# Residual rows with bias laid out in tile order in DRAM during the scores, for a two-layer attention kernel on one Trainium2 core

## Chip, cores and metric

The kernel runs on one core of a Trainium2 chip. The time is the device time of one execution in microseconds (us). Three runs of the kernel before gave 3094.94, 3099.14 and 3100.99 us; the median is 3099.14 us. One further execution was recorded by the hardware profiler and took 3099.78 us. All views below are of that execution, and times within it count from its first instruction. The engines are called PE (TensorE; PEld is its weight load), DVE (VectorE), ACT (ScalarE), POOL (GpSimd) and SP (SyncE, which here only issues DMAs).

## What is computed

There are N = 2708 rows of D = 1024 features in x and a matrix adj of N x N integers. Two attention layers follow each other, each on the normalised rows and each with a residual:

```
h = max(layernorm(x), 0)
f = h @ Wf + bf ;  g = h @ Wg + bg
e = max(f @ g.T, 0)
attention = softmax(where(adj > 0, e, -9e15), axis=1)
x = x + attention @ (h @ W + bW)              # layer 0

h = max(layernorm(x), 0)
hW = h @ W1 ;  e = leaky_relu(hW @ a1 + (hW @ a2).T, 0.2)
attention = softmax(where(adj > 0, e, -9e15), axis=1)
x = x + max(attention @ hW, 0)                # layer 1
```

All is in 32-bit floats. The rows of attention add up to 1, so the kernel adds bW to the residual row instead of to h @ W. The sum x + bW for the rows of layer 0 is what this change is about.

## The kernel before

**Panels and tiles.** The output rows are worked on in five panels of 512 rows (panels 0 to 4). Panels 0 and 1 have 64 rows more each and panel 2 has 20 more; these 64 + 64 rows form a tile called MONO and the 20 rows one called TINY. A tile has 128 rows in four groups of 32: group g of tile t of a panel holds rows that begin at `start_of_tile(t) + 128 * g`, so that the rows of one tile are not neighbours in x. `places[t]` lists, for each group, the partitions and the first row. `pairs` joins two tiles; there are ten pairs, q = 0 to 9, and MONO with TINY comes after them.

**Stages of a layer-0 panel p.** (1) `project_q` (PE names qx, qy, qz) makes the operand B of the scores. (2) `scores` multiplies it with the transposed rows of all ten pairs. For each q it loads four blocks As (hs_d to SBUF, in `product`, matmul at L1378), builds the mask for pair q + 1 (integers of adj are loaded, converted and turned on DVE, stored to mk_d by GpSimd), and adds mask and maximum on DVE. (3) The softmax runs beside later matmuls. (4) `aggregate` (gx, gy, gz, gv at L661) multiplies the weights with h; the division by the row sums is at L977, partly on GpSimd. (5) `project` (px, py, pz, pv at L1267) multiplies with W and hands each half tile to `finish0`, which adds it to the residual row, stores the sum to x1_d and makes the normalised rows for layer 1. The products are cut in Strassen's manner into seven (M1 to M7). Panel p's projection comes after its aggregation for p = 0, 1, 2 and 4; panel 3's comes after the scores of panel 4.

**The residual rows.** `finish0(p).start` runs when `project` begins, after the first four loads of W and ahead of all others. For each tile of the panel it takes two half rows of 512 columns, x_res, in SBUF. `load_rows_of` fills them by eight loads of 32 rows x 512 columns (64 KB) from x; MONO takes four of 64 rows, TINY sixteen small ones. Then two DMAs on GpSimd add the bias row, repeated on 128 partitions, into x_res (L1612; for TINY eight at L1607). `go` and `join` add the projected rows to it.

**What sets the order.** All loads go through `load`, which issues on SP and keeps the order of the program. Stores go through `store` on GpSimd; a scheduler may move them unless they are kept in order too. `nc.hold` keeps DVE's instructions in order during the scores. Side work (statistics of finished rows, masks, quarter sums) waits in the lists `later` and `lazy` and is taken by `behind(us)` after each product. Tiles in SBUF come from pools: `slots` (54 buffers, x_res among them) and `strm` (12 buffers: As, W blocks w, hc, adj_i, g1 and g2). A load waits for the release of its buffer, and so does everything behind it on SP. The built order also shows that a DMA waits for the one eight places before it among the DMAs of the same engine.

Of the kernel before, what the change touches and what calls it, by code (L numbers as in the profile page):

```python
# [57 lines left out]
def kernel(  # L58
# [66 lines left out]
    def slot(name, shape=(P, WX), dt=FP):  # L125
        return slots.tile(list(shape), dt, tag="slot", name=name)
# [10 lines left out]
    def load(o, i):  # L137
        for a, b in in_16(o, i):
            tc.keep_in_program_order(nc.sync.dma_start(a, b))
# [146 lines left out]
    def by_quarters(a, r, e):  # L286

        return [(slice(B32 * g, B32 * g + NY), a[r:r + NY, e * W + g * P:e * W + (g + 1) * P]) for g in range(P // B32)]
# [1064 lines left out]
    def scores(p, B):  # L1353

        w = width[p]
        h = w // 2
        lo, hi = slice(0, h), slice(h, w)
        fetch, convert, turn = makers[p]
        rb = slot("rb")
        if p == 0:  # L1360
            spread(rb, columns_of(p, r_[:, first_col[p]:]))
        else:
            row_on_all(rb, r_d[p], p)
        acc = slot("acc")
        S = [None] * NT
        rates = (0.6, 1.0, 0.65, 0.65, 0.65)
        lefts = {}

        def product(q, m, ps, start):
            n, i = P, BY_SCORES.index(m)  # L1370
            if i % 2 == 0:
                t = stream("As", (P, 2, NH, P))
                lefts[q] = t
                k = min(2, 7 - i)
                load(t[:, :k].rearrange("p m c j -> p (m c j)"),
                     hs_d[q][:, i:i + k].rearrange("p m c j -> p (m c j)"))
            for c in range(NH):
                nc.tensor.matmul(ps[:n, :h], lefts[q][:, i % 2, c, :n], B[m][c // 2][:, c % 2, :h],  # L1378
                                 start=(start and c == 0), stop=(c == NH - 1), skip_group_check=True)

        def finish(q, s, k):

            n, mk = once(q, k), mk_sb[p, q]
            nc.vector.scalar_tensor_tensor(s[:, :w], s[:, :w], 0.0, mk[:, k, :w], op0=OP.max, op1=OP.add)
            if q == 0 and k == 0:
                nc.vector.tensor_copy(acc[:, :w], s[:, :w])
            else:
                nc.vector.tensor_tensor(acc[:n, :w], acc[:n, :w], s[:n, :w], OP.max)
            if q in known:
                raise_max(p, q, k, mk[:n, k, :w])  # L1390

        def last(q, sb, Z, m1):

            n = P
            product(q, M4, Z, False)
            add(sb[:n, lo], Z[:n, :h], m1[:n, lo])
            finish(q, sb, 1)
            mk_sb.pop((p, q))
            behind(rate, True)

        nc.hold = ("vector",)
        left_over = None
        for q in range(NQ):
            n = P
            make_until(q + 2)
            rate = 1.3 if NQ - 1 not in made else rates[p]
            if q + 2 <= LEFT:
                fetch(q + 2)
            sa, sb = slot("Sa"), slot("Sb")
            S[pairs[q][0]], S[pairs[q][1]] = sa, sb  # L1410
            X, Y, Z = (bank(f"s{k}") for k in "xyz")
            m1, t = slot("sm1"), slot("st")
            product(q, M1, X, True)
            for s in (lo, hi):
                add(m1[:n, s], X[:n, :h], rb[:n, s])
            if left_over:
                left_over()
            product(q, M6, Z, True)
            add(t[:n, lo], Z[:n, :h], m1[:n, hi])
            behind(rate, True)  # L1420
            product(q, M5, Y, True)
            add(t[:n, hi], Y[:n, :h], m1[:n, hi])
            if q + 1 <= LEFT:
                convert(q + 1)
            behind(rate, True)
            product(q, M2, X, False)
            add(sa[:n, lo], X[:n, :h], rb[:n, lo])
            if q + 1 <= LEFT:
                turn(q + 1, 0)
            behind(rate, True)  # L1430
            product(q, M7, Z, False)
            add(sb[:n, hi], Z[:n, :h], t[:n, hi])
            if q + 1 <= LEFT:
                turn(q + 1, 1)
            behind(rate, True)
            product(q, M3, Y, False)
            add(sa[:n, hi], Y[:n, :h], t[:n, lo])
            finish(q, sa, 0)
            behind(2 * rate, True)
            left_over = lambda q=q, sb=sb, Z=Z, m1=m1: last(q, sb, Z, m1)  # L1440

        sm, st = slot("Sa"), slot("Sb")
        S[MONO], S[TINY] = sm, st
        X, Y, Z = (bank(f"s{k}") for k in "xyz")
        m1, zs = slot("sm1"), slot("sz")
        t = stream("As", (P, 2, NH, P))
        load(t.rearrange("p e c j -> p (e c j)"), hsl_d.rearrange("p e c j -> p (e c j)"))

        def part(ps, e, m, start):
            for c in range(NH):  # L1450
                nc.tensor.matmul(ps[:, :h], t[:, e, c], B[m][c // 2][:, c % 2, :h], start=(start and c == 0),
                                 stop=(c == NH - 1), skip_group_check=True)
        part(X, 0, M1, True)
        add(m1[:, hi], X[:, :h], rb[:, hi])
        left_over()

        for c in range(NH):
            for g, (e, m) in enumerate(((0, M1), (1, M2), (0, M5), (1, M3))):
                nc.tensor.matmul(Z[B32 * g:B32 * (g + 1), :h], tinyT[:, e, c], B[m][c // 2][:, c % 2, :h], start=(c == 0),
                                 stop=(c == NH - 1), skip_group_check=True)  # L1460
        nc.scalar.copy(zs[:, :h], Z[:, :h])
        part(X, 1, M2, False)
        add(sm[:, lo], X[:, :h], rb[:, lo])
        behind(rate, True)
        part(Y, 0, M5, True)
        part(Y, 1, M3, False)
        add(sm[:, hi], Y[:, :h], m1[:, hi])
        finish(LEFT, sm, 0)
        for s, pick in zip((lo, hi), picks):
            V = bank("sv")  # L1470
            nc.tensor.matmul(V[:, :h], pick, zs[:, :h], start=True, stop=True)
            add(st[:, s], V[:, :h], rb[:, s])
        finish(LEFT, st, 1)
        mk_sb.pop((p, LEFT))
        behind(rate, True)
        nc.hold = ()
        return S, acc
# [110 lines left out]
        nc.gpsimd.memset(t, 0.0)  # L1588
        return [t[:, e] for e in range(2)]

    def bias_of_W(o, n, k):
        return bass.AP(tensor=bw.tensor, offset=bw.offset + o, ap=[[0, n], [1, k]])

    def finish0(p):
        xs, seen = {}, {}

        def start(ts):
            for t in ts:
                if p == NP - 1:
                    first_mask[t] = load_mask(0, *pair_of[t])  # L1600
                if t == TINY:
                    xs[t] = halves_of_tiny("x_res")
                    for e in range(2):
                        for ps, i in by_quarters(x, places[TINY][0][1], e):
                            load(xs[t][e][ps], i)
                        for g, (ps, _) in enumerate(by_quarters(x, 0, e)):
                            nc.gpsimd.dma_start(xs[t][e][ps], bias_of_W(e * W + g * P, NY, P), accum_op=OP.add)  # L1607
                    continue
                xs[t] = row_halves("x_res", t == MONO)
                load_rows_of(t, xs[t], x)  # L1610
                for e in range(2):
                    nc.gpsimd.dma_start(xs[t][e], bias_of_W(e * W, P, W), accum_op=OP.add)  # L1612

        def go(t, e, c):
            add(xs[t][e], c, xs[t][e])
            if t == TINY:
                for ps, o in by_quarters(x1_d[t], 0, e):
                    store(o, xs[t][e][ps])
            else:
                store(x1_d[t][:, e * W:(e + 1) * W], xs[t][e])  # L1620
            seen[t] = seen.get(t, 0) + 1
            if seen[t] == 2 and t == TINY:
                put(0.5, lambda: rows_of_tiny())
            elif seen[t] == 2:
                rows_done(t, xs[t])

        def rows_of_tiny():
            xs[TINY] = row_halves("x_res")
            for e in range(2):
                nc.gpsimd.memset(xs[TINY][e], 0.0)  # L1630
                for ps, _ in places[TINY]:
                    nc.gpsimd.dma_start(xs[TINY][e][ps], x1_d[TINY][:, e * W:(e + 1) * W])
            rows_done(TINY, xs[TINY])

        def join(t, e, c):
            add(xs[t][e], xs[t][e], c)
        return start, join, go
# [199 lines left out]
```

## Time and profile before

| what | value |
|---|---|
| median of three runs | 3099.14 us |
| profiled execution | 3099.78 us |
| its span, first to last instruction | 3098.0 us |
| DVE, ACT and POOL busy | 2070.7, 463.2, 506.3 us |
| mean granted clock of PE | 0.989 of full speed |
| mean DMA rate | 247 GB/s |
| scores of panels 1, 2, 3, 4 | about 661, 1074, 1452, 1771 us to 812, 1212, 1590, 1902 us |
| projections of panels 0 to 4 begin | about 611, 1012, 1399, 1902, 2085 us |

How to read the views. "Busy" is the time in which an engine executed; waiting and issuing DMAs are not counted. The waits of an engine name the instruction that waited, what released it, and the total, the number and the longest. A timeline row has the start, the length, the engine, the line and the operation, and in brackets the idle time before it with its releaser. A row of a stretch has the length, the busy time of PE, PEld, DVE, ACT and POOL (each with its number of instructions), the mean granted clock of PE as a share of full speed, the mean busy share of the 16 DMA engines, and their rate in GB/s. In names, a buffer's number is left out, so x_d stands for every x1_d tile; "SPq" is SP's DMA queue.

### The profile page before, as it was taken

The numbers are of one execution on the slowest core, as the hardware profiler recorded it, in microseconds if no ns is written. First come the engines' busy times: TensorE is split into PE (matmuls) and PEld (weight loads), VectorE is DVE, ScalarE is ACT, GpSimd is POOL, SyncE is SP. The second block draws the span as 40 slices with busy tenths as digits, with TensorE's granted clock in tenths as the row PEclk, the third lists the DMA queues.
The fourth block names the chain that finished last, engine by engine and source line by source line (L and its number), as shares of the span: only waits on it lengthen the run. The fifth ranks groups of instructions, "written<-read, shape, count | busy, mean of one in ns | idle before, by whom it ended". The sixth has DMA issues, their size and how long they took to land.

```text
span 3098.0 us, 41680 instructions
## 1 busy us (share of the span) xinstructions
PE 3002.8 (97%) x14630; PEld 2298.1 (74%) x14630; DVE 2070.7 (67%) x4615; ACT 463.2 (15%) x817; POOL 506.3 (16%) x786
## 2 busy tenths in 40 slices
PE   8998999899999999999999999997999999999998
PEld 4576777657877588885888886783777969879694
DVE  5767693776651596716975277766968768887853
ACT  3420020010110101101011001301222121212200
POOL 1421101310011110214101001141202010020202
PEclk9999999999999999999999999998999999999999
DMA  6999967998565796758967577789667868888896
GB/s 225 291 257 254 301 247 253 309 274 229 178 238 153 217 260 223 244 158 241 278 199 255 164 217 234 237 266 350 229 216 249 274 202 296 287 269 294 264 297 246
DMA packets 448577, 764.70 MB, mean 247 GB/s; under 512 B 175776, under 2 KB 262592, under 8 KB 448368
## 3 DMA queue, kind: packets, MB, share of 16 engines
q1 hardware_dynamic: 393008, 598.31, 62.0%
q0 software_dynamic: 55360, 163.73, 16.4%
q8 instruction: 116, 1.90, 0.3%
q14 instruction: 93, 0.76, 0.1%
HBM read 627.95 MB, written 133.91 MB: 246 GB/s over the span
## 4 chain that ended last, share of the span: by engine, by line
PE 71%; DVE 11%; DMA 7%; issue 7%; SPq 2%; POOL 1%; ACT 1%; POOLq 0%; DVEq 0%; ACTq 0%
PE sz L1378 6%; PE gx L661 6%; PE gy L661 6%; PE gz L661 5%; PE gz L1067 5%; PE pz L1267 4%; PE sx L1378 4%; PE sy L1378 4%; PE px L1267 4%; PE py L1267 3%; PE gx L1067 3%; PE gy L1067 3%; PE M_ps L574 3%; PE qz L661 2%; PE qx L661 2%
## 5 line engine op out<-in xcount | busy, mean ns | idle before, releaser
L1378 PE MATMUL sz<-B,As 128*128 128x288 f32 (+2 forms) x1200 | 293.5, 394 | 11.8 <-DVE st L45 8.8
L1378 PEld LDWEIGHTS sz<-B,As 128*128 128x128 f32 x1200 | 227.8, 191 | 61.8 <-DVE st L45 12.7
L1378 PE MATMUL sx<-B,As 128*128 128x288 f32 (+2 forms) x800 | 199.6, 392 | 6.4 <-DMA As<-hs_d 4.4
L1378 PE MATMUL sy<-B,As 128*128 128x288 f32 (+2 forms) x800 | 199.3, 392 | 2.3 <-DMA As<-hs_d 2.3
L661 PE MATMUL gz<-Sa,hc 128*128 128x288 f32 (+2 forms) x800 | 189.2, 397 | 6.3 <-DMA hc<-hg_d 6.3
L661 PEld LDWEIGHTS gz<-Sa,hc 128*128 128x128 f32 x800 | 153.8, 193 | 40.1 <-DMA hc<-hg_d 6.8
L1378 PEld LDWEIGHTS sx<-B,As 128*128 128x128 f32 x800 | 151.3, 190 | 40.1 <-DMA As<-hs_d 3.7
L1378 PEld LDWEIGHTS sy<-B,As 128*128 128x128 f32 x800 | 152.0, 190 | 33.4 <-issue 2.7
L1067 PE MATMUL gz<-quarter,hc 128*128 128x128 f32 (+2 forms) x1344 | 168.8, 279 | 3.8 <-DVE gT L45 3.7
L143 POOL DMA_DIRECT2D out_dram<-x_res x180 | 89.0, 501 | 482.1 <-DVE x_res L45 474.7
L1067 PEld LDWEIGHTS gz<-quarter,hc 128*128 128x128 f32 x1344 | 160.6, 191 | 5.1 <-DVE gT L45 4.6
L1267 PE MATMUL px<-w,gT 128*128 128x512 f32 x320 | 143.9, 602 | 7.5 <-DMA w<-in_L_gnn_W_dram 6.0
L1267 PE MATMUL pz<-w,ps 128*128 128x512 f32 x320 | 142.1, 594 | 0.8 <-DVE pt L45 0.8
L1267 PE MATMUL py<-w,ps 128*128 128x512 f32 x320 | 142.0, 593 | 0.0
L143 POOL DMA_DIRECT2D mk_d<-mask x55 | 35.8, 652 | 534.8 <-DVE mask L45 528.1
L1267 PEld LDWEIGHTS px<-w,gT 128*128 128x128 f32 x320 | 60.9, 193 | 80.9 <-issue 74.7
L1267 PEld LDWEIGHTS pz<-w,ps 128*128 128x128 f32 x320 | 60.2, 190 | 77.1 <-issue 70.7
L1267 PEld LDWEIGHTS py<-w,ps 128*128 128x128 f32 x320 | 60.5, 190 | 75.8 <-issue 73.9
L574 PE MATMUL M_ps<-wgT,wfT 128*128 128x512 f32 x256 | 113.5, 600 | 1.6 <-ACT hsT L45 1.6
L661 PE MATMUL gy<-T,hc 128*128 128x288 f32 (+2 forms) x480 | 111.6, 394 | 0.0
L977 POOL TENSOR_TENSOR gT<-gT,rr 128x2304 f32<-128x2304 f32 (+5 forms) x12 | 44.4, 3700 | 382.4 <-DVE rr L45 179.8
L661 PEld LDWEIGHTS gy<-T,hc 128*128 128x128 f32 x480 | 91.2, 190 | 19.5
(377 smaller groups left out, 5803.6 us busy)
## 6 DMA issues: line engine op xcount, KB each, us to landing
hc<-hg_d SPq DMA_DIRECT2D x175, 512.0 KB
As<-hs_d SPq DMA_DIRECT2D x150, 512.0 KB
hc<-hr_d SPq DMA_DIRECT2D x119, 512.0 KB
hc<-hs_d SPq DMA_DIRECT2D x112, 512.0 KB
w<-wt_d SPq DMA_DIRECT2D x96, 512.0 KB
w<-in_L_gnn_W_dram SPq DMA_DIRECT2D x72, 512.0 KB
md<-md_d SPq DMA_DIRECT2D x56, 512.0 KB
adj_i<-in_adj_dram SPq DMA_DIRECT2D x200, 128.0 KB
```

Source lines behind the costliest of these rows:

```text
L143: nc.gpsimd.dma_start(a, b)
L574: nc.tensor.matmul(ps, wfT[a][c // NH][:, c % NH, :], wgT[b][c], start=(c == 0), stop=(c == NC - 1))
L661: nc.tensor.matmul(ps[d], left(m, k, d), right(m, k), start=(start and k == 0), stop=(k == K - 1), skip_group_check=True)
L977: nc.gpsimd.tensor_tensor(of(e, s), of(e, s), by(s, k), OP.mult)
L1067: nc.tensor.matmul(ps[:, d], lhs[:, d * P:(d + 1) * P], inner_right(m, n, k), start=(start and k == 0 and d == 0), stop=(k == NK - 1), ski ...
L1267: nc.tensor.matmul(ps, left[i][m][:, k, :], w_[k], start=(start and k == 0), stop=(k == NH - 1), skip_group_check=True)
L1378: nc.tensor.matmul(ps[:n, :h], lefts[q][:, i % 2, c, :n], B[m][c // 2][:, c % 2, :h], start=(start and c == 0), stop=(c == NH - 1), skip_g ...
```

## The change

For panels 1 to 4 the sum x + bW is made in DRAM, in the order of the tiles, in the tensors x1_d[t], which before only took the result of layer 0. In the scores of panel p, at q = 2, GpSimd issues one DMA per tile that copies the tile's rows from x to x1_d[t] (two for MONO, one for TINY). At q = 6 it issues one accumulating DMA per tile that adds the bias row to x1_d[t]. Both are kept in GpSimd's order of the program. In `finish0.start` a tile is then loaded from x1_d[t] by two loads of 128 rows x 512 columns (256 KB) with no accumulate after them. TINY keeps its sixteen small loads, now from x1_d. Panel 0 stays as it was.

```diff
@@ scores(p, B)
             if q + 2 <= LEFT:
                 fetch(q + 2)
+            if p and q in (2, 6):
+                (copy_residual if q == 2 else bias_residual)(p)
@@ beside finish0
-    def bias_of_W(o, n, k):
-        return bass.AP(tensor=bw.tensor, offset=bw.offset + o, ap=[[0, n], [1, k]])
+    def tiles_of(p):
+        return list(full(p)) + ([MONO, TINY][p - 1:p] if p in (1, 2) else [])
+
+    def by_gpsimd(o, i, **k):
+        tc.keep_in_program_order(nc.gpsimd.dma_start(o, i, **k))
+
+    def copy_residual(p):
+        for t in tiles_of(p):
+            if t < MONO:
+                r = places[t][0][1]
+                by_gpsimd(x1_d[t].rearrange("(g r) c -> g r c", g=P // B32),
+                                    bass.AP(tensor=x.tensor, offset=x.offset + r * D, ap=[[P * D, P // B32], [D, B32], [1, D]]))
+            else:
+                for ps, r in places[t][:1] if t == TINY else places[t]:
+                    by_gpsimd(x1_d[t][:NY] if t == TINY else x1_d[t][ps],
+                                        x[r:r + ps.stop - ps.start, :])
+
+    def bias_residual(p):
+        for t in tiles_of(p):
+            n = NY if t == TINY else P
+            by_gpsimd(x1_d[t], bass.AP(tensor=bw.tensor, offset=bw.offset, ap=[[0, n], [1, D]]), accum_op=OP.add)
@@ finish0.start
                     for e in range(2):
-                        for ps, i in by_quarters(x, places[TINY][0][1], e):
+                        for ps, i in by_quarters(x1_d[t], 0, e):
                             load(xs[t][e][ps], i)
-                        for g, (ps, _) in enumerate(by_quarters(x, 0, e)):
-                            nc.gpsimd.dma_start(xs[t][e][ps], bias_of_W(e * W + g * P, NY, P), accum_op=OP.add)
                     continue
                 xs[t] = row_halves("x_res", t == MONO)
-                load_rows_of(t, xs[t], x)
+                if p == 0:
+                    load_rows_of(t, xs[t], x)
                 for e in range(2):
-                    nc.gpsimd.dma_start(xs[t][e], bias_of_W(e * W, P, W), accum_op=OP.add)
+                    if p == 0:
+                        nc.gpsimd.dma_start(xs[t][e], bass.AP(tensor=bw.tensor, offset=bw.offset + e * W, ap=[[0, P], [1, W]]),
+                                            accum_op=OP.add)
+                    else:
+                        load(xs[t][e], x1_d[t][:, e * W:(e + 1) * W])
```

## Prediction

> **What bounds the kernel now.** I read the page's busy shares first, then the waits of TensorE (PE), then, for the one long wait there, the timelines of PE and of SyncE's DMA queue (SP) and the stretches around it.
>
> ```profile
> PE 3002.8 (97%) x14630; PEld 2298.1 (74%) x14630; DVE 2070.7 (67%) x4615; ACT 463.2 (15%) x817; POOL 506.3 (16%) x786
> ...
> PE sz L1378 <- DVE st L45: 8.8, 8, 2.2
> PE mx_ps L849 <- DVE mx L45: 8.3, 1, 8.3
> ...
> PE gz L661 <- DMA hc<-hg_d: 6.3, 1, 6.3
> PE px L1267 <- DMA w<-in_L_gnn_W_dram: 6.0, 1, 6.0
> ```
>
> PE is busy for 3002.8 of 3098.0 us, so 95 us of idle is all that an edit without matmuls can touch. The waits (columns: total, times, longest) name one that the residual loads can cause: 6.0 us before px at L1267, the projection of layer 0, for a block of W. None is for x_res. The wait for hg_d belongs to panel 0, the 8.3 us for mx to the chain after the last tile of layer 0.
>
> ```profile
> 2085.15 3.60 PE L1267 MATMUL px<-w,gT 128*128 128x512 f32 x8
> 2088.59 3.60 PE L1267 MATMUL py<-w,ps 128*128 128x512 f32 x8
> 2098.14 6.29 PE L1267 MATMUL px<-w,gT 128*128 128x512 f32 x8 [5.96 <-DMA w<-in_L_gnn_W_dram]
> 2104.27 3.60 PE L1267 MATMUL pz<-w,ps 128*128 128x512 f32 x8
> ```
>
> This is panel 4. Eight matmuls take 3.44 us from start to start (2085.15 to 2088.59); those after the wait take 6.13 (2098.14 to 2104.27). So the wait costs 5.96 us and then 6.13 - 3.44 = 2.7 us more. The stretches show why, in the granted clock (second last but one column):
>
> ```profile
> 2092.00:2098.00 6.00, 0.18 (x1) 0.00 (x0) 1.99 (x3) 0.00 (x0) 0.86 (x1) 0.88 1.10 259
> 2098.00:2105.00 7.00, 6.86 (x10) 2.92 (x11) 0.53 (x1) 0.00 (x0) 0.00 (x0) 0.61 1.06 364
> ```
>
> The block was late because of SP, which issues in order:
>
> ```profile
> 2054.56 2.82 SPq L139 DMA_DIRECT2D w<-wt_d  x2
> 2057.47 1.45 SPq L139 DMA_DIRECT2D maskl<-mk_d  x1
> 2058.97 7.89 SPq L139 DMA_DIRECT2D x_res<-in_x_dram  x8
> 2067.05 0.34 SPq L139 DMA_DIRECT2D maskl<-mk_d  x1
> 2067.84 5.95 SPq L139 DMA_DIRECT2D x_res<-in_x_dram  x8
> 2074.08 0.34 SPq L139 DMA_DIRECT2D maskl<-mk_d  x1
> 2074.70 5.52 SPq L139 DMA_DIRECT2D x_res<-in_x_dram  x8
> 2080.38 0.34 SPq L139 DMA_DIRECT2D maskl<-mk_d  x1
> 2080.83 7.90 SPq L139 DMA_DIRECT2D x_res<-in_x_dram  x8
> 2088.77 1.82 SPq L139 DMA_DIRECT2D w<-in_L_gnn_W_dram  x2
> ```
>
> The 32 loads of 64 KB hold SP for 7.89 + 5.95 + 5.52 + 7.90 = 27.3 us; W goes out at 2088.77 and lands at 2098.0, 9.2 us later. [...]
>
> In the projections of panels 1 to 3 (stretches 1005 to 1075, 1390 to 1460, 1895 to 1955) PE is busy for 70.0 of 70, 68.6 of 70 and 60.0 of 60 us, with no wait for W: the same loads are hidden there.
>
> [...]
>
> **The change, part by part.**
>
> Removed on SP: 148 loads from x. Added: 50 loads from x1_d, 34 of 256 KB (16 small ones for TINY are exchanged one for one). For panel 4 it is 8 for 32. Loads of that size from x1_d exist in layer 1: 329 ns at the median to issue, 852 at most. In the built order SP's loads around them stand as before, so what holds SP is read from its waits: the third and fourth mask loads and the fourth tile wait until the first two pairs of quarter sums (hs_d<-hq) are stored. GpSimd issues those at 2059.8 and 2063.6, two each, 0.73 us apiece, and they land 6.9 us later (median), so by about 2072. Eight loads at 0.33 to 0.85 us are 3 to 7 us and end inside that. W for px goes out at about 2072, its buffer free since gz ended at 2064, and with the same 9.2 us lands at 2081 to 2082: ten us ahead of PE, which is there at 2092.03. So 5.96 + 2.7 = 8.7 us go.
>
> What is late next? The following blocks wait for buffers that gv frees between 2068 and 2085, the seventh for px at 2088.6 with 17 us to its use; loads in this stretch land in 9 to 10 us. So none. The 0.78 us wait for pt at 2108.64 stays, as VectorE must empty the bank first, and the 8.3 and 3.9 us at 2143 to 2157 hang on the last tile and move with it.
>
> Removed on GpSimd: 42 bias accumulates of panels 1 to 4 (34 of 256 KB, 0.94 us to issue at the median, and with panel 0's 42.8 us of waiting for loads). Nothing on PE waited for them; VectorE lost 2.5 us, beside PE's wait. Cost off the path: zero. In panels 1 and 2 the second scaling of gT (L977) no longer stands behind an accumulate; PE didn't wait for it either.
>
> Added on GpSimd: 19 copies at q = 2 and 18 accumulates at q = 6. By the nearest rows, 0.5 to 0.75 us to issue a store and 0.94 (to 2.25) for an accumulate: 3 us and 5 us (to 11) per panel. Queued behind are mask stores, and in panels 1 and 2 stores of layer-1 rows (hr_d). GpSimd is idle for 10 to 13 us before each late mask store, and the bias comes 50 us after the copy it waits for, so this is hidden. If hr_d<-g is late, SP waits for its stream buffer (7.4, 1.9 and 14.7 us in the scores of panels 1 to 3, with no PE wait for it).
>
> Added DMA traffic: 2.1 to 2.6 MB copied per panel, then 2.1 MB of bias added in DRAM. At the 400 GB/s of the stretch 2105 to 2116 (402) a copy burst is 5 to 6.5 us of all engines, the bias 5 us, or 10.5 if read and write-back count apart. These are estimates. What it may hit is the scores' loads of As:
>
> ```profile
> 1141.33 2.83 SPq L139 DMA_DIRECT2D As<-hs_d  x4
> 1152.78 2.08 SPq L139 DMA_DIRECT2D As<-hs_d  x4
> ...
> 1150.00:1163.00 13.00, 13.00 (x60) 11.02 (x59) 8.18 (x18) 0.00 (x0) 0.96 (x2) 1.00 1.07 234
> ```
>
> In panel 2 the pair that PE starts at 1150.3 has its loads issued at 1141.33, the next (1162.9) at 1152.78: 9 to 10 us ahead. GpSimd's stores there land in 5.2 us; if loads are like them, 4 us are slack. The DMA share is 1.07 just where the bias falls. In panel 1 the lead is 9 to 11 us at the copy and 14 at the bias, in panel 3 14 and 9, in panel 4 over 20. So three bursts fall on a thin cover: copy of panel 1, bias of 2 and 3. Each costs from 0 (it shares the engines by turns and is over within the slack) to 6.5 us (10.5 less 4). I take 0.3 us each, 1 us in all, since no load of As was late in panels 1 to 4 although the share is over 1 in several stretches; both ends stay in the range.
>
> Moved: the built order puts VectorE's statistics and dots of panel 3 later in panel 4's aggregation, and three transposes earlier in its projection. PE is busy for 10.00 of 10 us in every stretch from 1955 to 2055: zero, at worst 2 us.
>
> **Sum.** -8.7 + 1 = -7.7 us against the profiled execution's 3099.78 (span 3098.0 and 1.8 around it): 3092.1. The median of the runs is 3099.14, 0.6 lower, so 3091.4. A difference below 0.2% (6.2 us) can't be told from none here; faster means below 3092.9.
>
> **Rivals.**
> 1. Paid back in part: the three thin bursts cost 1 to 3 us each, 3 to 9 in all: 3094 to 3100. For it: the leads of 9 us. Against: none of these loads was late.
> 2. The stall moves: W comes in time but a later block or VectorE's emptying holds PE for 3 to 5 of the 8.7 us, or SP is held longer by the quarter sums: 3093 to 3097. For it: 402 to 409 GB/s from 2105 on. Against: the accumulates leave this stretch, and the later blocks keep their distance to PE.
> 3. Slower: adding bias in DRAM goes at half rate and takes turns with As in panels 1 to 3: 10.5 us less 4 of slack, three times, 19.5 us; with -8.7 that is +10.8, 3110. It decides once the bursts put off As by over 15 us in all. For it: shares of 1.05 to 1.12 in stretches of the scores of panels 2 and 3. Against: those shares go with 234 to 336 GB/s, while over 400 were moved after 2105.
> That the copies don't happen, or that SP still issues the small loads, is excluded by the built order.
>
> **Chances.** Forecast 0.57; rival 1 0.20; rival 2 0.10; rival 3 0.13. The first is faster, the next two within 0.2%, the last slower. The range runs from 3086 (no cost, 5 us of scatter as in the three runs) to 3104, past rivals 1 and 2; it leaves out rival 3 and a little below.
>
> **What would show it.** Right: px at 2098 no longer waits for W, the clock there stays at 1.00, and W's issue is some 16 us earlier against the end of gv. As: no wait of sx, sy or sz for hs_d in panels 1 to 4. The forecast is wrong if such waits add up to more than 2 us, if px still waits, or if a pair of panels 1 to 3 takes longer with As in time.

## The result, and the profile after

The changed kernel takes 3131.09 us at the median of four runs (3127.59 to 3133.11), the kernel before, with one more run, 3100.06 (3094.94 to 3103.75). The ratio is 1.010, with a 95% interval of 1.0082 to 1.0118: about 31 us slower. The forecast was 3091.4 with a range of 3086 to 3104, so the sign was wrong and the range missed. The profiled execution of the changed kernel took 3127.59 us, its span is 3125.8.

PE's line on the page and PE's longest wait (columns: total, times, longest) of the changed kernel:

```profile
PE 3011.2 (96%) x14630; PEld 2306.7 (74%) x14630; DVE 2070.6 (66%) x4615; ACT 460.4 (15%) x815; POOL 494.7 (16%) x781
...
PE sx L1378 <- DMA As<-hs_d: 37.3, 5, 11.6
```

The wait of px for W has left the list, and a new one leads it: sx for As, 37.3 us. Of these, 10.9 us belong to panel 0, which the change leaves as it was (its waits for As under all three names are 13.5 us, for 9.1 before); 26.4 are new, in panels 1, 2 and 3. PE is also busy for 8.4 us more with the same number of matmuls.

What was to go has gone. PE's timeline at the start of panel 4's projection, after:

```profile
2119.19 3.60 PE L1267 MATMUL px<-w,gT 128*128 128x512 f32 x8
2122.62 3.60 PE L1267 MATMUL py<-w,ps 128*128 128x512 f32 x8
2126.06 3.60 PE L1267 MATMUL px<-w,gT 128*128 128x512 f32 x8
2129.49 3.60 PE L1267 MATMUL pz<-w,ps 128*128 128x512 f32 x8
```

The second px follows py without a gap, 3.44 us after it, and pz follows 3.43 us later; the granted clock from 2119 to 2133 is 1.00. SP's queue shows why:

```profile
2092.69 1.39 SPq L139 DMA_DIRECT2D x_res<-x_d  x2
...
2094.70 1.02 SPq L139 DMA_DIRECT2D x_res<-x_d  x2
...
2101.73 0.81 SPq L139 DMA_DIRECT2D x_res<-x_d  x2
...
2105.28 1.20 SPq L139 DMA_DIRECT2D x_res<-x_d  x2
2107.98 2.39 SPq L139 DMA_DIRECT2D w<-in_L_gnn_W_dram  x2
```

Eight residual loads hold SP for 1.39 + 1.02 + 0.81 + 1.20 = 4.4 us instead of 27.3, and W goes out at 2107.98, 18 us ahead of its use. In the kernel before, SP waited 14 times from 2055 to 2092, 5.4 us in all, for a residual load to land, each time for the DMA eight places earlier in its queue.

What came instead is in the scores. SP's queue in panel 2, first in the kernel before:

```profile
1155.62 6.87 SPq L139 DMA_DIRECT2D adj_i<-in_adj_dram  x8
...
1166.38 5.67 SPq L139 DMA_DIRECT2D As<-hs_d  x8
```

and in the changed kernel:

```profile
1153.99 3.74 SPq L139 DMA_DIRECT2D adj_i<-in_adj_dram  x4
1157.83 3.88 SPq L139 DMA_DIRECT2D adj_t<-in_adj_dram  x4
1161.81 3.26 SPq L139 DMA_DIRECT2D As<-hs_d  x4
1166.54 18.82 SPq L139 DMA_DIRECT2D adj_i<-in_adj_dram  x8
1185.46 3.77 SPq L139 DMA_DIRECT2D adj_t<-in_adj_dram  x8
1189.27 4.45 SPq L139 DMA_DIRECT2D As<-hs_d  x8
```

The eight adj_i loads are the integers for the mask of MONO with TINY; they stand on SP ahead of the next blocks of As. Before the change the stretch of their issues was 6.87 us long, now it is 18.82. GpSimd issued the bias of panel 2 at 1161.54, just ahead of them. As goes out at 1189.27, and PE, which was ready at 1186.2 (1193.36 less 7.12), waits:

```profile
1184.28 1.96 PE L1378 MATMUL sy<-B,As 128*128 128x266 f32 x8
1193.36 3.92 PE L1378 MATMUL sx<-B,As 128*128 128x266 f32 x8 [7.12 <-DMA As<-hs_d]
```

The stretches of that time (last three columns: granted clock, DMA share, GB/s):

```profile
1190.00:1196.00 6.00, 2.65 (x6) 2.11 (x7) 0.00 (x0) 0.00 (x0) 0.00 (x0) 0.61 0.89 296
1196.00:1203.00 7.00, 7.00 (x27) 5.72 (x27) 2.98 (x6) 0.00 (x0) 0.00 (x0) 0.84 0.96 348
```

Eight matmuls after the wait take 3.92 us, not 1.96, and the granted clock over these 3.92 us is 0.50. The slow clock after a wait, which the prediction had counted for px (6.13 us for 3.44), is paid at the other new gaps too: 4.21 us for 2.10 in panel 1 and 3.38 for 1.89 in panel 3. In panel 1 the wait is 7.66 us, behind 24.59 us of adj_i; in panel 3 it is 11.64 us, behind the four adj_i loads of an ordinary pair:

```profile
1551.70 13.32 SPq L139 DMA_DIRECT2D adj_i<-in_adj_dram  x4
1565.07 4.86 SPq L139 DMA_DIRECT2D As<-hs_d  x4
...
1574.23 3.38 PE L1378 MATMUL sx<-B,As 128*128 128x256 f32 x8 [11.64 <-DMA As<-hs_d]
```

Panel 4 has the slow adj_i loads (19.44 us), but its As are over 20 us ahead, and no wait.

The DMA engines show what slowed SP's queue (a row: packets, MB, share of the 16 engines; q0 carries GpSimd's DMAs, q1 SP's). In panel 2 the four As issued at 1161.81 stand ahead of the eight adj_i loads. They are 1.84 MB. The same four blocks passed in 6 us in the kernel before (1154 to 1160):

```profile
q1 hardware_dynamic: 1094, 1.87, 94.1%
```

In the changed kernel they took the 17 us from 1163 to 1180:

```profile
q1 hardware_dynamic: 655, 1.84, 40.4%
```

From 1165 to 1180 the bias was in flight all the time:

```profile
q0 software_dynamic: 507, 1.87, 69.8%
q1 hardware_dynamic: 498, 1.34, 32.2%
```

The engines moved 498 of SP's packets and 507 of GpSimd's: nearly one for one. But a packet of q0 took 0.698 x 16 x 15 us / 507 = 0.33 us and one of q1 0.155. The small packets of the adj_i loads came behind: from 1180 to 1187 SP's queue moved 4196 packets, 124 bytes each at the mean. In panel 3 it is the mask loads that took the turns, from 1555 to 1565:

```profile
q0 software_dynamic: 444, 1.65, 92.3%
q1 hardware_dynamic: 436, 0.15, 9.7%
```

Again one for one, though SP's packets were 0.34 KB at the mean and GpSimd's 3.7 KB. So in these stretches what stood in SP's queue, large packets or small, advanced by about one packet for each accumulate of 4 KB. The counts agree with turns; how long one turn is they don't show.

The stages, from PE's first matmul of one to that of the next, in us against the kernel before (one profiled execution each):

| run | scores p1 | scores p2 | scores p3 | projection p4 |
|---|---|---|---|---|
| before (length) | 151.9 | 138.6 | 137.8 | 75.8 |
| after | +10.3 | +9.8 | +13.2 | -9.7 |
| copy_only | -2.3 | 0.0 | +0.4 | -9.7 |
| bias_overwrites | +1.3 | +6.5 | +9.2 | -9.7 |
| bias_from_128_rows | +6.9 | +9.5 | +12.7 | -9.7 |
| panel_4_only | -2.2 | 0.0 | -0.3 | -9.7 |
| one_tile_per_pair | +7.6 | +24.1 | +9.5 | -9.7 |
| bias_at_q3 | +13.7 | +10.2 | +13.1 | -9.7 |
| bias_at_q8 | -0.1 | 0.0 | -0.2 | -9.7 |
| mask_loads_behind_As | +1.4 | +7.9 | +4.5 | -9.7 |
| third_W_first | +0.1 | 0.0 | -0.3 | +1.8 |
| panel_4_bias_at_q8 | +0.2 | 0.0 | +0.5 | -9.7 |

The span grew by 27.8 us: 33.3 in the three scores, -9.7 in the projection, 4.2 in all else. 2.3 of these 4.2 lie behind the last store: from the end of its issue to the end of the span it is 8.9 us, before the change 6.6. The eight runs that change panels 1 to 3 have 7.8 to 9.0 us there, the other four 6.0 to 6.6; so the work for these panels has a small price at the end too, and why is not shown. Up to the scores of panel 1, ahead of the copies and the bias, the runs scatter by more: these scores begin between 646 and 661 us.

### The profile page after: what moved, and what is told of

The parts are those of the page before. It is cut to its first block, busy times and chain, and to the rows that moved or that the text cites. A ratio compares the mean times of both kernels' runs of the same rounds, so it can differ in the third digit from the quotient of the medians.

```text
span 3125.8 us, 41412 instructions
## 1 busy us (share of the span) xinstructions
PE 3011.2 (96%) x14630; PEld 2306.7 (74%) x14630; DVE 2070.6 (66%) x4615; ACT 460.4 (15%) x815; POOL 494.7 (16%) x781
## 4 chain that ended last, share of the span: by engine, by line
PE 72%; DVE 10%; issue 7%; DMA 7%; SPq 3%; POOL 1%; ACT 1%; POOLq 0%; DVEq 0%; ACTq 0%
PE sz L1378 6%; PE gx L661 6%; PE gy L661 6%; PE gz L661 5%; PE gz L1067 5%; PE sx L1378 4%; PE pz L1267 4%; PE px L1267 4%; PE sy L1378 4%; PE py L1267 3%; PE M_ps L574 3%; PE gx L1067 3%; PE gv L661 3%; PE gy L1067 3%; SPq L139 3%
## 5 line engine op out<-in xcount | busy, mean ns | idle before, releaser
L1378 PE MATMUL sx<-B,As 128*128 128x288 f32 (+2 forms) x800 | 208.8, 406 | 39.3 <-DMA As<-hs_d 37.3
L661 PEld LDWEIGHTS gy<-T,hc 128*128 128x128 f32 x480 | 91.2, 190 | 19.5
```

Source lines behind the costliest of these rows:

```text
L661: nc.tensor.matmul(ps[d], left(m, k, d), right(m, k), start=(start and k == 0), stop=(k == K - 1), skip_group_check=True)
```

## The experiments

The theory after the result: the bias, added in DRAM during the scores, holds the DMA engines and delays SP's mask loads, which stand ahead of As. The rivals: the copies do it; any burst of that size does it, added or not; 128 reads of one bias row are slow because they hit one place; and, for the remedy, the size of one burst, its place beside the mask loads of MONO and TINY, or the sum of the added DMA time decides. Each ratio below is against runs of the kernel before that were taken beside the experiment (medians 3095.9, 3096.6 and 3098.48 us), with a 95% interval.

**copy_only.** The bias isn't added in panels 1 to 4.

```
-            if p and q in (2, 6):
-                (copy_residual if q == 2 else bias_residual)(p)
+            if p and q == 2:
+                copy_residual(p)
```

> The changed kernel without its bias accumulates (panels 1 to 4 get no bias; bW is all zeros here). Theory A, the bias bursts hold the DMA engines in front of the loads of As: the three waits of sx for As (7.7, 7.1 and 11.6 us) and the slow clock after them go, the gain at the last projection stays, 3091 to 3094 us. Theory B, the copies' bulk is at fault as much as the bias: at least a third of the 26 us of waits stays, 3100 to 3120 us.

Measured: 3090.4 us, against the kernel before 0.998 (0.997 to 0.9989). PE's waits for As are 12.2 us, all in panel 0:

```profile
PE sx L1378 <- DMA As<-hs_d: 12.2, 2, 9.7
```

So the copies cost PE nothing, although they wrote as many bytes; the whole loss is the bias. That is not for want of load on the engines. In panel 2, from 1103 to 1109:

```profile
DMA packets 432, 2.72 MB, mean 453 GB/s; under 512 B 116, under 2 KB 301, under 8 KB 400
q0 software_dynamic: 213, 2.48, 105.1%
q1 hardware_dynamic: 219, 0.24, 11.2%
```

The copies of the four whole tiles, 2.1 MB, went in 32 packets of 64 KB (432 less 400), the shares of the two queues add up to 116%, and SP's queue got 219 packets through. But that was over in 6 us; the bias with its packets of 4 KB held SP's queue for some 17.

**bias_overwrites.** The bias row is written over the residual rows and not added, so the residual of panels 1 to 4 is left out.

```
-            by_gpsimd(x1_d[t], bass.AP(...), accum_op=OP.add)
+            by_gpsimd(x1_d[t], bass.AP(...))
```

> The changed kernel with the same bias DMAs as plain copies: they overwrite the rows of x1_d instead of adding (the residual of panels 1 to 4 is lost). Same bytes read and written, no read-back. Theory A1, it is adding in DRAM that is slow: the burst is half as long, the waits for As fall from 26 us to 0 to 10, 3091 to 3106 us. Theory A2, it is any burst of 2.1 to 2.6 MB at this place, or the reading of one row 128 times: waits of 20 us or more, 3118 to 3131 us.

Measured: 3109.85 us, 1.0041 (1.0027 to 1.0054). The waits for As in panels 1 to 3 are 1.2, 4.3 and 7.4 us, 12.9 for 26.4:

```profile
768.92 2.21 PE L1378 MATMUL sx<-B,As 128*128 128x288 f32 x8 [1.19 <-DMA As<-hs_d]
...
1552.76 3.78 PE L1378 MATMUL sx<-B,As 128*128 128x256 f32 x8 [7.40 <-DMA As<-hs_d]
```

About half of the waits come with a burst of such packets at this place, though nothing is added; the other half come with the adding.

**bias_from_128_rows.** The bias is read from 128 copies of the row in DRAM, made at the start, instead of 128 times from one row.

```
+    bw_d = dram.tile([P, D + 64], FP, name="bw_d")
+    nc.gpsimd.dma_start(bw_d[:, :D], bass.AP(tensor=bw.tensor, offset=bw.offset, ap=[[0, P], [1, D]]))
...
-            by_gpsimd(x1_d[t], bass.AP(...), accum_op=OP.add)
+            by_gpsimd(x1_d[t], bw_d[:n, :D], accum_op=OP.add)
```

> The changed kernel with the bias read from 128 different rows in DRAM (made once at the start) instead of one row 128 times. Theory A3, all engines read the same 4 KB and that is slow: bursts land in half the time, waits for As fall below 12 us, 3091 to 3110 us. Theory A1, adding in DRAM is slow: no change, 3126 to 3134 us.

Measured: 3122.52 us, 1.0082 (1.0069 to 1.0096); waits for As of 6.4, 6.0 and 9.5 us, 21.9 in all. The one row isn't the cause; whether the 4.5 us less are its part or scatter stays open.

**panel_4_only.** Copy and bias in DRAM for panel 4 alone; panels 0 to 3 as in the kernel before.

```
-            if p and q in (2, 6):
+            if p == NP - 1 and q in (2, 6):
...
-                if p == 0:
+                if p < NP - 1:
```

> Copy and bias in DRAM for panel 4 alone, panels 0 to 3 as in the kernel before. If the gain of the change lies in the last projection and its cost in the scores of panels 1 to 3: px no longer waits for W (6.0 us and 2.7 us of slow clock), no wait for As in panels 1 to 4, 3089 to 3093 us. If the gain at panel 4 hangs on something else: 3098 to 3101 us.

Measured: 3084.27 us (3084.09 to 3085.23), 0.996 (0.9948 to 0.9973): 0.4% faster than the kernel before. The gain at px is kept (-9.7), no As is late. So the whole benefit sits in panel 4, and the work for panels 1 to 3 buys nothing, as the prediction read from their projections.

**one_tile_per_pair.** The same work in portions: copies at q = 1 to 5, bias at q = 4 to 8, one tile each.

```
-            if p and q in (2, 6):
-                (copy_residual if q == 2 else bias_residual)(p)
+            if p and 1 <= q <= 5:
+                copy_residual(p, q - 1)
+            if p and 4 <= q <= 8:
+                bias_residual(p, q - 4)
...
-        for t in tiles_of(p):
+        for t in tiles_of(p)[i:i + 1]:
```

> The changed kernel with the same copies and the same adding of bias, but one tile per pair of the scores: the copies at q = 1 to 5, the bias at q = 4 to 8. In the changed kernel 4 to 5 bias DMAs at once (40 to 50 packets of 4 KB on each DMA engine at about 0.29 us each) held back the mask loads in front of As by some 17 to 20 us, more than the lead of As. Size of the burst decides: now each burst is 8 to 10 packets on each engine, about 3 us of delay per pair, less than the lead of 9 to 17 us: no wait for As in panels 1 to 4 over 1 us in all, no half clock after it, 3085 to 3092 us. Amount decides (the bytes to be added cost DMA time that the scores don't have): the same 2.1 to 2.6 MB per panel is only spread, waits of 10 to 30 us remain in all, 3105 to 3131.

Measured: 3133.1 us, 1.0119 (1.0102 to 1.0136), no better than the change. Panel 2 alone has three long waits in place of one:

```profile
1132.85 3.56 PE L1378 MATMUL sx<-B,As 128*128 128x266 f32 x8 [5.03 <-DMA As<-hs_d]
1143.94 3.91 PE L1378 MATMUL sy<-B,As 128*128 128x266 f32 x8 [3.94 <-DMA As<-hs_d]
...
1199.58 3.92 PE L1378 MATMUL sx<-B,As 128*128 128x266 f32 x8 [6.47 <-DMA As<-hs_d]
```

So my theory that the size of one burst against the lead of As decides falls. A sum of the shares was the next thing to try: does the amount decide? In the scores of panel 2 GpSimd's queue took 12.1% of 138.6 us before, 17.0% of 138 in copy_only and 24.1% of 148 after, that is 16.8, 23.5 and 35.7 us of all engines: 6.7 for the copies, 12.2 for the bias. The kernel before, from the first pair to the last loads of As of panel 2, had

```profile
1084.00:1174.00 90.00, 87.89 (x390) 73.56 (x389) 78.50 (x179) 3.49 (x6) 11.49 (x16) 1.00 0.92 248
```

a DMA share of 0.92. With a share of 1 taken as the limit (an estimate of mine; single stretches show up to 1.10), some 7 us were to spare in 90. The copies just fit in that; copies and bias are 12 us too many, and 9.8 were lost; for bias_overwrites (21.9% of 145 us) 15 were added, 8 too many, and 6.5 were lost. So the sum fits three runs in panel 2. It does not fit this one: the portions add the same work and cost 24.1 us in that panel. Why is not explained. Nor does it fit mask_loads_behind_As below, with the same work and 13.8 us lost in three panels instead of 33.3. That the amount decides is not shown.

**bias_at_q3.** Copies at q = 0 and bias at q = 3.

```
-            if p and q in (2, 6):
-                (copy_residual if q == 2 else bias_residual)(p)
+            if p and q in (0, 3):
+                (copy_residual if q == 0 else bias_residual)(p)
```

> The changed kernel with copies at q = 0 and bias at q = 3, so that the burst meets the mask loads of an ordinary pair (4 + 4 loads with rows of 256 bytes) instead of the 8 + 8 loads with rows of 128 bytes for MONO and TINY. Place decides (only the many small packets of MONO and TINY suffer from taking turns): waits for As in panels 1 to 3 of at most 3 us in all, 3085 to 3092 us. Turns alone decide (any small loads ahead of As are put off by the whole burst, about 17 us, and the lead there is 9 to 17 us): waits of 3 to 8 us in each of panels 1 to 3, 3103 to 3125.

Measured: 3127.18 us, 1.0103 (1.0085 to 1.0121). The waits only moved to earlier pairs, in panel 1 for example to

```profile
724.03 4.21 PE L1378 MATMUL sx<-B,As 128*128 128x288 f32 x8 [11.77 <-DMA As<-hs_d]
```

So it isn't the company of MONO and TINY that makes the bias costly.

**bias_at_q8.** Bias at q = 8 instead of 6, that is when SP has issued nearly all As of the panel.

```
-            if p and q in (2, 6):
+            if p and q in (2, 8):
```

> The changed kernel with copies at q = 2 as in it, and bias at q = 8, behind the mask loads of MONO and TINY and behind As of the pairs 8 and 9. Place or turns before As: SP has only the last loads of As and the loads of hT and md left, so no wait for As in panels 1 to 3; unless hT or md are then late for the stages after the scores, 3085 to 3092 us. Amount decides (the burst costs wherever it stands): 10 us or more of waits, now for hT, md, hc or the first loads of the next stage, 3103 to 3131.

Measured: 3090.3 us, 0.9984 (0.9974 to 0.9995). No wait for As in panels 1 to 3. SP's queue in panel 2:

```profile
1148.84 8.26 SPq L139 DMA_DIRECT2D adj_i<-in_adj_dram  x8
...
1161.96 5.60 SPq L139 DMA_DIRECT2D As<-hs_d  x8
...
1173.03 19.96 SPq L139 DMA_DIRECT2D hT<-hs_d  x8
```

The bias goes out at 1167.62, and now the loads of hT are the slow ones. By the counts of 1173 to 1188 the turns are the same as ever:

```profile
q0 software_dynamic: 584, 2.10, 71.7%
q1 hardware_dynamic: 581, 1.52, 32.8%
```

But hT and md are needed later, and no stage after is longer. The same burst, the same turns, no cost: it matters what SP still has to load that PE needs soon.

**mask_loads_behind_As.** Bias at q = 6 as in the change; the mask loads for pair q + 2 are issued behind the first three product steps of pair q.

```
-            if q + 2 <= LEFT:
-                fetch(q + 2)
...
             if q + 1 <= LEFT:
                 convert(q + 1)
+            if q + 2 <= LEFT:
+                fetch(q + 2)
```

> The changed kernel (copies at q = 2, bias at q = 6) with one edit: in every pair the mask loads for pair q + 2 are issued on SP after the first three product steps of pair q and not ahead of them, so that the loads of As for q stand ahead of those mask loads. Queue position decides (As is late because it stands behind mask loads that take turns with the bias): As waits of panels 1 to 3 fall from 26.4 to under 8 us in all; the mask loads have some 10 us less until they are converted, and if that is too little the waits come back as VectorE's (sx or sz for sm or st), up to 7 us per panel: 3088 to 3112 us. Full DMA engines decide wherever As stands: As waits of 20 us or more remain, 3118 to 3135.

Measured: 3097.46 us, 0.9991 (0.9981 to 1.0001). The waits for As in panels 1 to 3 are 2.63, 4.67 and 2.91 us, and one of 0.56 in panel 3:

```profile
753.99 3.57 PE L1378 MATMUL sz<-B,As 128*128 128x288 f32 x8 [2.63 <-DMA As<-hs_d]
...
1163.74 3.88 PE L1378 MATMUL sz<-B,As 128*128 128x266 f32 x8 [4.67 <-DMA As<-hs_d]
...
1541.60 5.38 PE L1378 MATMUL sz<-B,As 128*128 128x256 f32 x16 [2.91 <-DMA As<-hs_d]
```

10.8 us remain of 26.4, over the 8 that queue position allowed for and far under the 20 of full engines; the three stages lose 13.8 us and not 33.3. So with the same DMA work some 20 of the 33 us hang on which blocks of As stand behind mask loads on SP. What the rest hangs on stays open. It need not be full engines: in this order too one block of As, that of product M7, is the first behind the mask loads, and M7 is the step that waited in panels 1 and 2. In panel 2 SP's queue (the last line is the late blocks):

```profile
1138.92 13.42 SPq L139 DMA_DIRECT2D adj_i<-in_adj_dram  x2
1152.43 6.49 SPq L139 DMA_DIRECT2D adj_t<-in_adj_dram  x4
1159.21 3.41 SPq L139 DMA_DIRECT2D As<-hs_d  x4
```

The edit also reaches panel 0, and the scores of panel 1 begin at 646 us, 6 us earlier than in any other run here; so the whole time flatters this run, and the stages are the better measure.

**third_W_first.** The kernel before, without the change, with a third block of W ahead of the residual rows.

```
-        ws = {m: load_W(l, m) for m in order[:2]}
+        ws = {m: load_W(l, m) for m in order[:3 if by_pair and l == 0 else 2]}
```

> The kernel before (no copies, no bias in DRAM) with one edit: in layer 0 the third block of W is loaded ahead of the residual rows too, where the projection comes after its aggregation. If px of panel 4 waited because W stood behind 32 loads of residual rows on SP, the wait of 5.96 us at px goes; the fourth block, still behind them and issued at about 2090, is needed some 3.4 us later and may be late in its place by 2 to 3 us with the half clock after it: 3 to 8 us less than the kernel before, 3088 to 3094. If W was late for another reason (DMA engines full), the wait stays and the time is that of the kernel before within 3 us.

Measured: 3099.4 us, 1.001 (1.0001 to 1.002). The wait of px went, as SP's queue order demands, but the next blocks, still behind the residual rows, were late:

```profile
2089.25 3.60 PE L1267 MATMUL px<-w,gT 128*128 128x512 f32 x8
2095.26 3.33 PE L1267 MATMUL pz<-w,ps 128*128 128x512 f32 x4 [2.41 <-DMA w<-wt_d]
...
2106.04 2.04 PE L1267 MATMUL py<-w,ps 128*128 128x512 f32 x2 [4.72 <-DMA w<-in_L_gnn_W_dram]
```

The expected gain of 3 to 8 us didn't come. In the changed kernel the removal of the small loads did it; a better order of one block did not. An order with more blocks ahead was not run.

**panel_4_bias_at_q8.** As panel_4_only, with the bias at q = 8.

```
-            if p == NP - 1 and q in (2, 6):
+            if p == NP - 1 and q in (2, 8):
```

> Copy and bias in DRAM for panel 4 only, as in the run that left panels 0 to 3 as in the kernel before, with the bias at q = 8 instead of q = 6. Both positions had no wait for As in panel 4, so place does not matter there: within 0.2% of that run's 3084.3, 3080 to 3092 us. If the lower time of that run against the one with bias at q = 8 in all four panels (3090.3) was scatter of panel 0, this one falls between the two; if the extra loads and bursts of panels 1 to 3 cost some 6 us outside PE's waits, it stays at 3084 with a narrow spread.

Measured: 3090.88 us (3084.25 to 3095.38), 0.9974 (0.9966 to 0.9983). The stages of panels 1 to 4 are those of panel_4_only within 2.4 us; PE's idle time differs in panel 0, which neither touches. So the low 3084 of panel_4_only may in part be scatter, though its five runs lie within 1.2 us: the two intervals overlap (0.9966 to 0.9973), and a gain of about 0.3% is what both support. Between these two and bias_at_q8 the runs don't settle a best.

## Why the prediction was wrong

**The px stall: right.** 8.7 us were to go; the projection of panel 4 is 9.7 shorter. Most of the other 1.0 is the wait of 0.78 us for pt, which was to stay and went. W was to be issued 20 us ahead of its use (2072 to 2092); it was 18.

**What is late next: right.** No later block of W and no bank held PE there. third_W_first shows that this was not a matter of course: with the small loads still in place the stall does move on.

**GpSimd's issues: right.** 2.81 us for the copies and 4.3 for the bias per panel (3 and 5 taken); PE waits for no mask store.

**Work moved on VectorE: right.** Aggregation of panel 4 is 133.8 us for 133.6.

**"Added DMA traffic": the step that failed.** The prediction wrote of the three thin bursts: "I take 0.3 us each, 1 us in all, since no load of As was late in panels 1 to 4 although the share is over 1 in several stretches". Measured: 33.3 us in three scores, 26.4 of it waiting and 5.6 of the other 6.9 slow clock in the first eight matmuls after the gaps (2.1, 2.0 and 1.5 us more than eight took before them). The volume was not the error: the bias was bounded by 5 and 10.5 us per panel and took 12.2 in panel 2, the copies 5 to 6.5 and took 6.7 (for panel 1 the bias is 2.6 MB like the copy, not 2.1; that is a slip, and a small one). Three readings failed.

- The reason for "0.3" does not carry it. A DMA share near 1 with no load late says that the loads then in the queue came in time; it says nothing of what a further burst would do to those behind it.
- The lead was taken for each load of As by itself, 9 to 10 us less 5 of landing. But a load also waits for what stands ahead of it on SP. In panel 2 the late As were issued 12 us later (18.82 less 6.87 of adj_i), because the four blocks of As ahead of them on SP advanced packet for packet with the bias and the mask loads had to follow these. The four blocks took 17 us instead of 6, and PE still had them in time; what stood behind the mask loads was late. In panel 3 the mask loads took the turns themselves. mask_loads_behind_As gives back 20 of 33 us by order alone. The prediction had just used that same queue, SP in its order, for panel 4.
- The slow clock after a gap (2.7 us at px) was counted for the stall that goes and not for those that could come.

**Which bursts.** The prediction named the copy of panel 1 and the bias of 2 and 3. It was the bias of 1, 2 and 3; for panel 1 its 14 us of lead were thought enough.

**Rival 3 was right in kind:** bias at half rate putting off As in panels 1 to 3, given 19.5 us and a chance of 0.13. It was short by the same two terms: waits of 26.4 for 19.5, and no slow clock after them. That adding costs about twice a plain write is borne out by the waits (26.4 for 12.9); in time of the engines it was 1.5 times in panel 2 (last section).

## What to carry to other kernels

Before work is moved into "idle" DMA time, list what will stand in the other queues while it runs, how many packets the new burst has, and which load that the bound engine needs soon stands behind them. The lead of one load is not the slack of a queue: here 9 us of lead did not cover a burst that held the queue for 17, while one of 6 us cost nothing. The DMA share of a stage is a first look and no more; its sum fitted three runs here and failed for two. The same transfer was free two pairs later, when the loads behind it were for the next stage. And make a change only in the stage where the profile shows the wait: panel 4 alone carried all of the gain.

## What the runs showed of the hardware

Two queues with very different packets shared the DMA engines nearly one packet for one: 444 of GpSimd's to 436 of SP's in panel 3, with 1.65 and 0.15 MB; 507 to 498 and 584 to 581 where SP's packets were larger. So accumulates of 4 KB, at 0.33 us each, gave small loads about the rate of the accumulates. A copy inside DRAM with 64 KB packets shared them in the same way (213 to 219) and was over sooner, in 6 us for 2.1 MB. Accumulating in DRAM cost 1.5 times the engine time of only writing the same rows in panel 2: 12.2 us of all 16 engines against 8.3 for 2.2 MB. After idle gaps of 7 to 12 us the next eight matmuls took 1.8 to 2.0 times their time (3.92 us for 1.96 in panel 2, at a granted clock of 0.50). Cutting the burst in portions did not lower its cost at all: 3133.1 us for 3131.09.
